# A new order for the first third of a cross-attention and quantized feed-forward kernel

## The chip, the cores and the metric

The kernel runs on one core of one Trainium2 chip. A core has a tensor engine (TensorE, PE in the profile; its weight loads are PEld), a vector engine (VectorE, DVE), a scalar engine (ScalarE, ACT), a general engine (GpSimd, POOL) and a sync engine (SyncE, SP), which here issues all transfers. Each takes its own instructions in order; they wait for one another by semaphores. The metric is the time on the device in microseconds, as the median of several runs.

## The reference, cut to what matters

```python
x = x + xattn(layernorm(x), ctx, Wq, Wkv, Wout, bout)   # x: 4 x 2048 x 512, ctx: 4 x 154 x 512
x = x + ffn(layernorm(x), w1, b1, w2, b2, gamma, beta)  # 512 -> 2048 -> 512

# in xattn: 16 heads of 64; query i sees key j only where  j % 2048 == i
sim  = where(mask, q @ k.T * scale, max_neg); attn = softmax(sim)
out  = (attn @ v) @ Wout + bout
# in ffn: h = layernorm(x) * gamma + beta; then twice, around an exact gelu:
xq, sx = round(x * 127 / max|x|), ...           # by row
wq, sw = clip(round(w / mean|w|), -1, 1), ...   # one scale for a whole weight
y = (xq @ wq.T) / (sx * sw) + b
```

Query i < 154 sees exactly one key, its own, so its attention output is v of that key; a query from 154 on sees none, all its scores are alike, and its output is the mean of all v. The attention thus adds to x, in each batch, 154 different rows and then one row over and over. The weights of the feed-forward part become -1, 0 and 1, and the mean of |w| must be known before any of them can be made.

## The kernel before, in words

x is 64 tiles of 128 rows. They are numbered n in the order in which they are worked: in a batch the tiles 2 to 15 (which only get the mean row) come first, then tile 0 (`front`) and tile 1 (`second`). Everything is written out by hand, instruction by instruction, in three strings of words: BEGINNING (up to tile 23), STEADY (one round for four tiles, eight times) and ENDING (the last eight tiles). No planner runs; each word calls a small function, in the order of the string, and so sets the order on the queue of each engine. A word is letters and numbers; the table `words` near the end maps them. The ones that the text speaks of:

- `lo`, `lv`: load a block of Wout and of Wv (256 KB each, eight each). `w c`: eight instructions on TensorE that add block c of Wv times Wout into four banks; after `w7` the product W is complete, and `cw k` copies a quarter of it to SBUF (last number 1: VectorE, 0: ScalarE).
- `lc`: load the context (1232 KB). `sk k` sums its keys, `sf` spreads the first batch's mean, `mk` writes the means beside the last 26 keys of each batch, `lk` copies those keys.
- `pm`: mean row of batch 0 times W (bank `py_mean`); `Y b`: the first 128 keys of batch b times W (`py`); `pr`: the other keys and the means times W (`py_rest`). Each comes in two halves such as `Y0.0.2` and `Y0.2.4`, of four instructions (two blocks of K in f32). `y b`, `m` and `yr` read these banks on VectorE. The banks come from a pool of two (`ps_o`), which `W`, the second product of the feed-forward part, uses as well.
- `lw i.c`: load block c of w1 (i = 0) or of w2 (i = 1), 512 KB each, eight each. `ms i.c.v` sums its absolute values (v = 1 VectorE, 0 ScalarE), `z i.0` adds the eight sums, `z i.1` spreads the total by a product with ones on TensorE, `z i.2` makes the scale. `q i.c.v` turns a block into whole numbers, `c i.c.v` clips it to -1 to 1 (v = 1 VectorE, 0 GpSimd).
- `L i`: load a pair of x tiles. `lr`, `lb`: rows of bout, gamma, beta, b2 and halves of b1, spread over the partitions.
- For a tile n: `A`/`a` adds the attention's rows to x (VectorE / GpSimd); `S` takes mean and variance; `O`, `o`, `C` or `N` the reciprocal deviation of a group of tiles (`o` and `N` on GpSimd); `P`, `E` (VectorE) or `k`, `e` (GpSimd) or `P`, `g` the normalized rows; `R` their largest value and scale; `V`/`v` scales with w1's (`inv`, the "1 / d" by which b1 is multiplied); `Q` quantizes on ScalarE and `T` turns the tile by a transposing transfer on SP's queue.
- `I n.h.v`: the seed: half h of b1 times `inv` is written into the PSUM half in which the product then accumulates (v = 1 VectorE, 0 ScalarE). `U n`: the first product, 16 instructions of TensorE, 3.45 us. `G`: gelu of a half on ScalarE; `M`: its largest value on VectorE; `H`: quantization on ScalarE; `h`: the turn, on SP's queue; `W n`: the second product, 16 instructions; `D`, `X`/`x`, `F`, `f`: scale, b2, finish and store.

The PSUM halves of `I`, `U` and `G` come from a pool of three (`ps_h`), so a tile's second half is seeded only when a gelu of the tile before has read its own. The x pairs and the loaded blocks of w1 and w2 share a pool of 13 buffers (`ring`). An instruction's place on its queue is fixed; nothing overtakes.

Up to tile 0's product TensorE's order is `w0` to `w7` (with `z0.1` ahead of `w6`), `pm`, `Y0.0.2`, `Y2.0.2`, `Y0.2.4`, `z1.1`, `Y2.2.4`, `Y3.0.2`, `U0`, `Y3.2.4`, `U1`, `Y1` and `pr` by halves in turn, `U2`, `U3`, `W0`, `U4`, `W1`, `U5`, `W2`, `W3`, `U6`, `U7`, `W4`. The pieces that the change touches are these three strings alone; no function changes.

## Time and profile before

| | us |
|---|---|
| median of four runs (lowest, highest) | 513.13 (512.58, 513.32) |
| time of the profiled execution | 513.14 |
| its span | 511.0 |
| TensorE busy | 500.7 |
| VectorE, ScalarE, GpSimd busy | 424.5, 422.9, 390.6 |
| first product of tile 0 starts | 53.31 |
| last product ends, before the last finish and store | 506.99 |

The profile is of one execution. A row of the order of time has the start and the length in us, the engine, the line of the kernel, the operation, what it writes and reads (`out<-in`), the shape, how many instructions are merged in the row, and in brackets how long the engine stood idle before it and what ended that. TensorE's matmuls are pipelined and their ends modelled, so its slow stretches are read from the distances between weight loads and from the granted clock. An f32 product counts as two instructions per block of K. The function that all of TensorE's attention products share is line 470; `U` is line 560, `W` line 638, the seed line 552 (ScalarE) or 550 (VectorE), the whole numbers line 247 or 245, the clip line 250.

### The profile page before, as it was taken

The page shows a single profiled execution, that of the slowest core. Times are in us where ns is not written, and L with a number is a line of the kernel's source. Part 1 is how long each engine was busy: PE and PEld are TensorE (multiplying, and loading weights), DVE is VectorE, ACT ScalarE, POOL GpSimd, SP SyncE. Part 2 cuts the span into 40 slices and gives each one's busy share as a digit, 9 for nine tenths or more (in the row PEclk, how much of TensorE's full clock was granted, in tenths as well). Part 3 has the DMA queues.
Part 4 walks back from the last instruction along what each step waited for, and adds up shares of the span by engine and source line. Part 5 has one row for each costly group of instructions (what it writes and reads, how often), then busy time and mean ns, then how long its engine had stood idle before and what let it go on. Part 6 is the DMA issues. An engine that isn't in the chain of part 4 may idle for free.

```text
span 511.0 us, 6841 instructions
## 1 busy us (share of the span) xinstructions
PE 500.7 (98%) x2168; PEld 224.4 (44%) x2168; DVE 424.5 (83%) x768; ACT 422.9 (83%) x389; POOL 390.6 (76%) x499
## 2 busy tenths in 40 slices
PE   9997999999999999999999999999999999999996
PEld 3443444444444444444444444444444444444442
DVE  1388999898998999889899897989897989796751
ACT  1267999898998999898897997988888889989870
POOL 0049999999999999998998989798989788804020
PEclk9997999999999999999999999999999999999999
DMA  8998698566787976685978776968778694684644
GB/s 294 401 390 313 239 220 135 127 151 153 161 207 168 234 172 139 139 195 137 182 188 174 188 166 158 198 149 183 178 157 212 158 148 126 125 204 100 151 96 144
DMA packets 194111, 93.99 MB, mean 184 GB/s; under 512 B 170268, under 2 KB 170268, under 8 KB 194076
## 3 DMA queue, kind: packets, MB, share of 16 engines
q1 hardware_dynamic: 194076, 93.56, 75.7%
q8 instruction: 17, 0.28, 0.2%
q14 instruction: 18, 0.15, 0.1%
HBM read 34.55 MB, written 17.04 MB: 101 GB/s over the span
## 4 chain that ended last, share of the span: by engine, by line
PE 74%; POOL 13%; DMA 6%; DVE 3%; issue 1%; SPq 1%; ACT 1%; POOLq 0%; ACTq 0%; DVEq 0%
PE po L638 37%; PE ph L560 34%; POOL x L274 3%; DMA wo<-Wout_dram 3%; PE wps L441 2%; DMA x<-x_dram 1%; POOL h L331 1%; POOL h L332 1%; POOL w2q L250 1%; DMA hqT<-hq 1%; POOL r L297 1%; POOL x L354 1%; POOL h L328 1%; DVE m L591 1%; PE py_mean L470 1%
## 5 line engine op out<-in xcount | busy, mean ns | idle before, releaser
L560 PE MATMUL ph<-w1q,xqT 128*128 128x512 f16 x1024 | 230.2, 379 | 1.8 <-DVE ph L550 1.0
L638 PE MATMUL po<-w2q,hqT 128*128 128x512 f16 x1024 | 229.9, 379 | 0.5 <-DVE x L644 0.4
L591 DVE TENSOR_REDUCE m<-hid 128x1 f32<-128x1024 f32 (+1 forms) x130 | 152.7, 1191 | 30.8 <-ACT hid L579 30.6
L579 ACT ACTIVATE hid<-ph,d 128x1024 f32<-128x1024 f32 (+1 forms) x130 | 140.0, 1090 | 32.6 <-PE ph L560 25.1
L560 PEld LDWEIGHTS <-xqT 128*128 128x128 f16 x1024 | 100.1, 98 | 124.2 <-issue 4.3
L638 PEld LDWEIGHTS <-hqT 128*128 128x128 f16 x1024 | 99.9, 98 | 122.2 <-DMA hqT<-hq 1.7
L620 ACT ACTIVATE hq<-hid,i 128x2048 f16<-128x2048 f32 (+1 forms) x65 | 127.5, 1969 | 6.5 <-DVE i L608 1.9
L552 ACT ACTIVATE ph<-b_b,inv 128x1024 f32<-128x1024 f32 x92 | 101.4, 1113 | 2.3 <-POOL inv L374 0.8
L354 POOL TENSOR_TENSOR x<-x,b_b 128x512 f32<-128x512 f32 x58 | 72.8, 1271 | 0.0
L274 POOL TENSOR_TENSOR x<-x,mean 128x512 f32<-128x512 f32 x50 | 63.9, 1281 | 1.0 <-DVE mean L685 1.0
L332 POOL TENSOR_TENSOR h<-h,beta_b 128x512 f32<-128x512 f32 x46 | 58.8, 1279 | 3.6
L644 DVE SCALAR_TENSOR_TENSOR x<-po,d,x 128x512 f32<-128x512 f32 x64 | 47.4, 742 | 13.9 <-PE po L638 12.8
L331 POOL TENSOR_TENSOR h<-h,gamma_b 128x512 f32<-128x512 f32 x46 | 58.4, 1269 | 0.3
L613 POOL TENSOR_TENSOR d<-mh,wm 128x1 f32<-128x1 f32 x64 | 12.1, 192 | 56.7 <-DVE mh L606 52.8
L380 ACT ACTIVATE xqg<-h,s 128x512 f16<-128x512 f32 x64 | 45.3, 711 | 6.4 <-DVE s L368 3.1
L550 DVE TENSOR_SCALAR ph<-b_b,inv 128x1024 f32<-128x1024 f32 x36 | 45.8, 1271 | 0.0
L360 DVE TENSOR_REDUCE m<-h 128x1 f32<-128x512 f32 x64 | 41.6, 671 | 4.1 <-POOL h L332 3.9
L281 DVE BATCH_NORM_STATS2 bn<-x 128x6 f32<-128x512 f32 x64 | 43.4, 677 | 0.4 <-POOL x L274 0.4
L328 POOL TENSOR_SCALAR h<-x,minus,rstd 128x512 f32<-128x512 f32 x46 | 36.7, 801 | 1.1
L441 PE MATMUL wps<-wo,wv 128*128 128x512 f32 x64 | 29.4, 616 | 0.1
L250 POOL TENSOR_SCALAR w1q<-wi 128x1024 f16<-128x1024 int16 x5 | 5.3, 1060 | 29.9 <-ACT wi L247 27.3
L256 DVE TENSOR_REDUCE part<-ws 128x1 f32<-128x1024 f32 x6 | 7.0, 1212 | 18.9 <-DMA ws<-w1T_dram 18.9
(77 smaller groups left out, 289.7 us busy)
## 6 DMA issues: line engine op xcount, KB each, us to landing
x<-x_dram SPq DMA_DIRECT2D x32, 512.0 KB, 4.3
out_dram<-x SPq DMA_DIRECT2D x64, 256.0 KB, 2.4
ws<-w1T_dram SPq DMA_DIRECT2D x8, 512.0 KB, 8.1
ws<-w2T_dram SPq DMA_DIRECT2D x8, 512.0 KB, 10.1
wo<-Wout_dram SPq DMA_DIRECT2D x8, 256.0 KB, 8.1
wv<-WvT_dram SPq DMA_DIRECT2D x8, 256.0 KB, 3.4
ctx_sb<-ctxT_dram SPq DMA_DIRECT2D x1, 1232.0 KB
hqT<-hq SPq DMA_TRANSPOSE x65, 4.5
```

The lines of the kernel that those rows point to most:

```text
L274: e.tensor_tensor(x_of(n), x_of(n), y, ALU.add)
L331: nc.gpsimd.tensor_tensor(normed[n], normed[n], gamma_b, ALU.mult)
L332: nc.gpsimd.tensor_tensor(normed[n], normed[n], beta_b, ALU.add)
L354: e.tensor_tensor(x_of(n), x_of(n), b2_b, ALU.add)
L550: nc.vector.tensor_scalar(ph, row, d, None, ALU.mult)
L552: nc.scalar.activation(ph, row, AF.Identity, bias=0.0, scale=d)
L560: nc.tensor.matmul(bank[i], xqT[n][:, k, :], w1q[:, k, i * 512 : (i + 1) * 512], start=False, stop=(k == KD - 1), skip_group_check=True,)
L579: nc.scalar.activation(hidden[n][:, i * w : (i + 1) * w], up_ps[n][half][:, lo : lo + w], AF.Gelu, bias=0.0, scale=deq1[g][:, j : j + 1],)
L591: nc.vector.tensor_reduce(m2[:, i : i + 1], hidden[n][:, i * w : (i + 1) * w], AX.X, ALU.max, apply_absolute_value=True,)
L620: nc.scalar.activation(hq[n][:, lo : lo + w], hidden[n][:, lo : lo + w], AF.Identity, bias=0.0, scale=inv2[n],)
L638: nc.tensor.matmul(po, hqT[n][:, k, :], w2q[:, k, :], start=(k == 0), stop=(k == KH - 1))
L644: nc.vector.scalar_tensor_tensor(t, down_ps.pop(n), deq2[n], t, ALU.mult, ALU.add)
```

## The change

Only the order is other. In words:

- The w1 blocks come as 7, 3, 2, 0, 6, 4, 1, 5 instead of 5, 2, 6, 1, 3, 7, 4, 0. One block of w2 (5) is loaded ahead of w1's last, the context one block of Wv later, both halves of b1 ahead of tile 0's turn. w1's blocks are measured three on VectorE and five on ScalarE (five and three before).
- Seven of w1's eight clips are on GpSimd (four before) and two of W's quarters are copied by VectorE (none before). `mk` stands behind tile 0's sum `A0` (ahead of the mean `m` before).
- `Y3` is whole ahead of tile 0's product, and so is `pr`; `Y1` lies by halves behind tiles 0 and 1, `Y2` behind tile 2.
- Behind w2's scale, ScalarE makes five blocks of whole numbers (four before) ahead of tile 0's seeds `I0.0.0` and `I0.1.0`, and tile 1's `Q1` comes behind the second seed (between the two before).
- From tile 4 on, `U` and `W` alternate on TensorE (before, `W2 W3 U6 U7` and a few such pairs later). Some tiles change engine: `A18 A28 A29 A30 A34` become `a`, `a24 a31` become `A`, tiles 16, 18, 21 and 26 go by `P`, `g` instead of `k`, `e`, and tile 29 the other way.
- STEADY has its words in another order, with `U` and `W` alternating, and its `P`, `k`, `e` and `g` one tile on; ENDING has `D`, `H` and `X` at other places in the first three tiles.

```diff
     BEGINNING = """
-        lo0 lv0 lo1 lv1 lo2 lw0.5 lw0.2 lv2 lv3 w0 lw0.6 lw0.1 lo3 lv4 lw0.3 w1 ms0.2.1
-        lv5 lo4 ms0.5.1 lw0.7 w2 lw0.4 lw0.0 lo5 lv6 w3 lo6 lr0 lc lv7 w4 ms0.4.1 lo7
-        ms0.1.1 ms0.0.0 L0 lr1 ms0.3.1 ms0.7.0 w5 lw1.0 lw1.6 ms0.6.0 L1 z0.0 z0.1 w6 z0.2
-        q0.5.1 q0.4.0 lw1.2 sk2 lw1.5 q0.6.0 c0.4.0 sk0 lw1.7 sk1 q0.1.0 c0.6.0 w7 q0.3.1
-        lw1.4 xo0 q0.7.0 lw1.3 sk3 sf cw0.0 lw1.1 c0.3.1 cw1.0 c0.1.1 q0.0.1 lr2 pm0.2
-        cw3.0 lk q0.2.1 cw2.0 c0.7.1 ms1.0.0 L2 c0.2.0 pm2.4 ms1.6.1 ms1.2.0 lr3 c0.0.0 mk
-        Y0.0.2 m ms1.5.0 L3 A0 a3 S0 Y2.0.2 ms1.7.0 lb0 O0 P0 o0 ms1.4.0 a2 C0 Y0.2.4 S3
-        ms1.3.0 a1 S2 ms1.1.0 O2 c0.5.0 S1 O1 E0 o1 o2 z1.0 R0 z1.1 a5 Y2.2.4 z1.2 Q0 C1
-        a4 q1.5.0 T0 y0 a6 q1.4.0 O3 lb1 C2 Y3.0.2 q1.0.0 P1 V0 o3 E1 q1.1.0 a7 R1 I0.0.0
-        S4 c1.4.0 Q1 S5 X1 I0.1.0
-        U0 T1 C3 P3 q1.6.0 V1 L4 N4 L5 E3 L6 I1.0.0 L7 P2 Y3.2.4 L8 end G0.0 E2 k4 R2 G0.1
-        e4 M0.0 I1.1.0
-        U1 R3 Q2 G1.0 T2 y2 k5 y3 q1.3.0 Y1.0.2 V2 M0.1 a8 G1.1 L9 L10 pr0.2 V3 I2.0.0 S6
-        e5 R4 Q3 Y1.2.4 M1.0 I2.1.0 T3 a11 S8 H0 pr2.4 R5 c1.1.0 S7 h0
-        U2 I3.0.0 c1.0.0 M1.1 q1.7.0 a10 G2.0 yr c1.3.0 sr q1.2.0 I3.1.1 c1.7.0
-        U3 L11 Q4 c1.2.0 v4 y1 G2.1 T4 D0 N6 c1.5.1 c1.6.1 H1 P6 W0 M2.0 I4.0.0 a9 h1 M2.1
-        G3.0 a12 t1 I4.1.0
-        U4 S9 s0 k7 S10 Q5 N8 x0 H2 T5 P9 E6 W1 G3.1 D2 h2 e7 M3.0 G4.0 M3.1 I5.0.0 D1 g9
...
-        U5 F0 R6 H3 R7 k8 M4.0 V6 Q6 h3 e8 W2 F1 G4.1 S11 I6.0.0 T6 S12 X6 Q7 R8 f0 G5.0
-        T7 R9 X2 W3 M4.1 G5.1 f1 D3 a14 Q8 I6.1.0 M5.0 a17 H4 M5.1
-        U6 X4 N10 I7.0.0 A23 h4 F2 G6.0 x3 T8 H5 I7.1.1
...
+        lo0 lv0 lv1 lo1 lv2 lw0.7 lw0.3 lo2 lo3 w0 lw0.2 lv3 lw0.0 lo4 ms0.7.0 lw0.6 w1
+        ms0.3.1 lv4 lo5 lv5 w2 lw0.4 lv6 ms0.0.1 lw0.1 lw1.5 w3 ms0.6.0 lw0.5 lo6 lv7 lc
+        w4 ms0.4.1 lo7 lr0 ms0.1.0 L0 ms0.2.0 w5 L1 ms0.5.0 lw1.2 lr1 z0.0 lw1.0 z0.1 w6
+        z0.2 q0.7.1 q0.6.0 q0.4.1 q0.1.0 c0.6.0 sk0 lw1.6 lw1.3 sk1 q0.3.0 c0.1.0 lw1.1 w7
+        sk2 c0.7.0 q0.2.0 sk3 lw1.4 sf q0.5.0 c0.2.0 cw0.1 c0.4.0 lk cw1.0 lw1.7 pm0.2
+        cw2.0 xo0 ms1.5.1 q0.0.0 lr2 L2 cw3.1 pm2.4 c0.3.0 ms1.2.0 c0.5.1 c0.0.0 L3
+        ms1.0.0 Y0.0.2 m lb1 ms1.6.0 A0 a3 mk S0 Y0.2.4 L4 ms1.3.0 O0 P0 o0 ms1.1.0 lb0 a2
+        S3 Y3.0.2 C0 ms1.4.0 lr3 a1 S2 ms1.7.0 O2 S1 o2 E0 z1.0 R0 z1.1 a5 O1 Y3.2.4 Q0
+        z1.2 o1 P1 q1.2.0 T0 V0 P2 a7 q1.7.0 O3 y0 q1.0.0 C1 a4 pr0.2 C2 q1.6.0 o3 E1
+        q1.1.0 c1.7.0 R1 pr2.4 I0.0.0 E2 V1 c1.1.0 S4 I0.1.0
+        U0 S5 a6 Q1 R2 q1.5.0 T1 X1 y3 I1.0.0 C3 a8 Y1.0.2 end G0.0 yr N4 P3 I1.1.0 E3
+        U1 Q2 c1.5.1 S6 G0.1 T2 c1.0.0 R3 G1.0 L5 V2 M0.0 L6 k4 Y1.2.4 I2.0.0 e4 M0.1 Q3
+        q1.4.0 T3 M1.0 I2.1.0
+        U2 L7 k5 y1 e5 G1.1 v3 S7 H0 S8 Y2.0.2 N6 R4 I3.0.0 h0 c1.4.1 Y2.2.4 c1.6.1 M1.1
+        G2.0 k7 q1.3.0 c1.2.0 I3.1.1
+        U3 H1 D1 a9 R5 M2.0 c1.3.0 Q4 W0 G2.1 T4 P6 D0 V4 a10 G3.0 S9 sr h1 M2.1 I4.0.0
+        a14 Q5 N8 E6 I4.1.0
+        U4 s0 x0 T5 G3.1 P9 t1 F0 a11 I5.0.0 L8 y2 W1 H2 D2 R6 k8 M3.0 e7 G4.0 S10 h2 S11
...
+        U5 X2 R7 f0 G4.1 L9 M3.1 V6 Q6 e8 I6.0.0 T6 W2 M4.0 H3 F1 a12 M4.1 G5.0 h3 X4
+        I6.1.0
+        U6 F2 g9 Q7 S12 G5.1 T7 M5.0 N10 H4 s1 P10 W3 x3 M5.1 I7.0.0 h4 a13 G6.0 D3 R8 k11
+        f1 H5 I7.1.1
...
     STEADY = """
-        W-3
-        U0 I1.0.1 a12 S11 G0.0 N8 I1.1.0 M0.0
-        U1 Q2 P9 G0.1 T2 k8 G1.0 M0.1 k7 W-2 X3 I2.0.1 I2.1.0 G1.1 e7 F-3 Q3 f-3 H0 T3
...
+        U0 G0.0 W-3 I1.0.1 I1.1.0 G0.1 M0.0 Q2
+        U1 F-3 k7 T2 I2.0.1 X2 L14 G1.0 M0.1 e7 W-2 G1.1 R6 M1.0 I2.1.0 a13 R7 H0 a12 S11
...
     ENDING = """
-        U0 I1.0.1 k7 e7 W-3 G0.0 G0.1 M0.0 D-1 X1 I1.1.0 M0.1
...
+        U0 I1.0.1 G0.0 W-3 k7 G0.1 M0.0 e7 I1.1.0 M0.1 Q2
...
```

## The prediction

> **What bounds the kernel now.** I read the page's busy shares first, then the waits and the order of time of TensorE, then the stretches where it stands still.
>
> ```profile
> PE 500.7 (98%) x2168; PEld 224.4 (44%) x2168; DVE 424.5 (83%) x768; ACT 422.9 (83%) x389; POOL 390.6 (76%) x499
> ```
>
> TensorE is the bound: 98% busy, and the change adds and removes no product. Only time in which TensorE waits or runs slowly can be won or lost. TensorE in order of time, its bracketed idle times:
>
> ```profile
> 45.45 2.05 PE L230 MATMUL pt<-tot,ones 128*128 128x512 f32 x2 [2.87 <-DVE tot L224]
> ...
> 53.31 3.61 PE L560 MATMUL ph<-w1q,xqT 128*128 128x512 f16 x16 [0.35 <-ACT ph L552]
> ...
> 100.54 1.89 PE L560 MATMUL ph<-w1q,xqT 128*128 128x512 f16 x8 [0.44 <-ACT ph L552]
> 103.47 1.89 PE L560 MATMUL ph<-w1q,xqT 128*128 128x512 f16 x8 [1.05 <-DVE ph L550]
> ...
> 119.57 3.61 PE L638 MATMUL po<-w2q,hqT 128*128 128x512 f16 x16 [0.40 <-DVE x L644]
> ```
>
> The busy time by stretches (columns: stretch, length, PE, PEld, DVE, ACT, POOL, granted clock, DMA share, GB/s):
>
> ```profile
> 42.60:45.40 2.80, 0.00 (x0) 0.00 (x0) 2.66 (x9) 2.23 (x4) 2.59 (x3) 0.86 1.05 402
> 45.40:51.50 6.10, 6.05 (x7) 2.53 (x8) 4.59 (x16) 4.23 (x5) 6.10 (x8) 0.50 0.64 216
> ```
>
> The wait of 2.87 us for w2's total (z1.1) costs twice: behind it the clock is 0.50 for 6.1 us, which loses another 3.05. With 0.66 at 23.2 (weight loads 1.09 apart where 0.43 is usual, ending on a landing of Wout), 0.35 ahead of tile 0, 1.49 at tile 7 and 0.40 at 119.6, 8.8 us can be won at most. From 120 on TensorE has no gap. What it waits for in the front stands here (VectorE, ScalarE, GpSimd in order of time):
>
> ```profile
> 36.39 0.89 DVE L460 TENSOR_SCALAR ctx_rest<-sums 128x16 f32<-128x16 f32 x1
> 45.16 0.15 DVE L224 TENSOR_REDUCE tot<-part 128x1 f32<-128x8 f32 x1
> ```
> ```profile
> 43.85 1.06 ACT L262 ACTIVATE w2q<-ws 128x1024 f16<-128x1024 f32 x1 [0.17 <-DMA ws<-w2T_dram]
> ...
> 47.99 4.27 ACT L247 ACTIVATE wi<-ws,sw 128x1024 int16<-128x1024 f32 x4 [0.89 <-DVE sw L238]
> 52.16 1.10 ACT L552 ACTIVATE ph<-b_b,inv 128x1024 f32<-128x1024 f32 x1
> ```
> ```profile
> 35.09 2.15 POOL L250 TENSOR_SCALAR w1q<-wi 128x1024 f16<-128x1024 int16 x2 [2.65 <-DVE wi L245]
> 38.25 1.28 POOL L274 TENSOR_TENSOR x<-x,mean 128x512 f32<-128x512 f32 x1 [1.01 <-DVE mean L685]
> ```
>
> The last measured block of w2 lands at 43.85; the total follows at 45.16, behind an unbroken row of VectorE work.
>
> **The change part by part.**
>
> *Loads on SP's queue.* Waits show w1's last block landed at 22.50, Wout's sixth at 23.21, the context at 28.39: 0.65 us per 256 KB. The new order has w5's pair six such units earlier, so the 0.66 goes. But a block of w2 and the fifth w1 block now end w1's set four units later: 22.5 + 2.6 = 25.1, then 1.25 to measure (1.06 and the 0.19 read) and 0.16 for the total: 26.6. Before, that total ended at 25.92, with TensorE there at 26.75. The product z0.1 stays at about 26.75: nothing gained, and 0.2 lost at worst. The context lands 1.3 later (29.6); its four sums (0.74 each) and the spread (0.6) end at 33.2, then VectorE copies W's first quarter (cw0.1; the copies on ScalarE take 0.53, I take 0.6): 33.8, where TensorE is ready at 33.84. +0.06. Ahead of w2's last block stand 15,056 KB in both orders, so it lands at 43.85 again. Behind that block tile 0's turn (T0) had 8 units ahead of it on SP's queue (beta, b2, two x pairs, one half of b1); now it has 12 (both halves and a third pair): 43.85 + 12 x 0.67 = 51.9, and 2.4 to 2.7 us of its own, 54.6 at the latest. The seed below comes later, so it is hidden; without that cover it would cost 1.3 against 53.3. SP stands at T0 until 47.9, and behind it lie only T1 and later x pairs.
>
> *w1's clips.* GpSimd gets seven of eight instead of four (1.04 each), done at about 37.3: covered, since tile 3's sum (a3) waits for the mean until 38.3 anyway. Without that cover, 1 us of GpSimd.
>
> *mk, the mean of the keys.* It moves behind tile 0's sum, next to a3. Its row has 0.89 us for 16 elements and ends with the clip of GpSimd's row above (37.24). I read it as held by GpSimd: here until a3's end at 39.6, so tile 0's statistics start 0.9 later (39.7). Bounds: 0.15 (the small rows) to 1.3 (a whole a3). I take 0.9, from where a3 stands in the row. The Trainium skill, SBUF — State Buffer, section "SBUF: two separate sides", says VectorE's two-port operations and GpSimd lock one port pair for a whole instruction; by that rule lk and the clip c0.5.1, now beside GpSimd's clips, would wait up to 1.04 each too: all of it ahead of the mean at 37.5, so the sum stays.
>
> *The chain to z1.0.* Behind it o0 ends at 41.9, a2 and a1 (1.24 each) at 44.4, tile 1's statistics (0.82) and tile 0's affine (0.67) at 45.94. w2's total is then at 45.94 instead of 45.16, TensorE's z1.1 at 46.2 instead of 45.45. The products ahead of it are as many as before, so the wait grows to some 3.6. The clock came back at 51.5 before; if at the same moment, 0.4 of its loss returns. The Trainium skill, TensorE: Matmul & The Clock Gate, Part 1, halves the clock after an idle window of about 3.4 us; here 2.8 sufficed. By the rule alone only the longer wait would surely halve it, which adds nothing to a clock already halved.
>
> *Five blocks ahead of b1 / d.* w2's scale follows z1.1 by 2.5 us: 48.7. ScalarE then makes five blocks instead of four (1.04 each) and tile 0's first seed (1.04): 55.0 instead of 53.2. Tile 0's product starts at 55.1 instead of 53.31: +1.8.
>
> *The products of the rest.* Behind z1.1 and ahead of tile 0 stood two half products (Y2.2.4, Y3.0.2: four instructions each); now three (Y3.2.4, pr0.2, pr2.4). The third is 4 x 0.43 = 1.72 us of work that is no longer owed later (two of Y2 move behind tile 2 for it and for Y1's). pr0.2 needs the bank that y0 frees at about 50.9 and would be next at 50.7: 0.2, hidden too, since TensorE is done at 54.9 and the seed comes at 55.0. Net at tile 0: 1.8 - 1.72 = +0.1. If mk is not held, ScalarE is 0.8 earlier and TensorE itself the limit at 54.4: -0.6.
>
> *Up to tile 7.* Y1 and Y2 lie behind tiles 0, 1 and 2, so tile 2 comes 3.4 us earlier against its own inputs; its second seed ends at 67.4, needed at 67.2: +0.3. From 48.7 ScalarE has 8 blocks (1.04), 11 seeds (1.04), 10 gelus (1.0), 5 x (0.62) and 3 h (1.89): 38.7, to 87.7. GpSimd, from a3 at 38.3: 12 sums (1.24), 4 powers (3.5), 5 clips (1.02), scales 2.3, b2 1.24, 3 norms (3.0), 3 k/e (3.4) and a k, 0.5: 47.5, and 2.35 idle: tile 7's normal rows at 88.2, before 87.18:
>
> ```profile
> 85.94 1.27 POOL L332 TENSOR_TENSOR h<-h,beta_b 128x512 f32<-128x512 f32 x1
> ```
>
> TensorE now alternates W and U: W2, U6, W3, U7 where it had W2, W3, U6, U7. U6 is due at 93.4, three earlier, and its scales come at 89.3 to 90.4, its turn at about 93.5. ScalarE waits some 2 us at Q6 for them, and behind it on that queue stand both seeds of tile 6, h of tile 3 and a gelu: it seeds the second half by 95.7 (wait 0.5); h of tile 3 at 93.6 and 4.5 us (the row below, turns from issue to landing) give W3 at 98.1 (wait 0.6). In return tile 7 finds both seeds, its 1.49 is gone, and it ends at about 105.1 where it ended at 105.2. The later 0.40 hangs on a finish behind a held GpSimd; it may stay.
>
> ```profile
> DMA to landing us min/median/max: 4.2/4.5/5.7
> ```
>
> *The rest.* From tile 8 on three more tiles go by VectorE and GpSimd together (P, g), three sums cross back, the steady rows shift a P, k, e and g by one tile and the ending's two dequants wait for their words. TensorE's order at the end is the same, so the last 4.0 us are. I cost all this at nothing: other engines are 87 to 91% busy in that stretch, TensorE 100%. If that cover fails, one late seed (1.1) in each of eight steady rounds would be 9; nothing points there.
>
> **Sum.** Profiled 513.14 (span 511.0 and 2.1 around), 0.01 off the median. +0.1 at tile 0, +0.3 at tile 2, +0.4 -0.9 at tiles 6 and 7 (to -0.1 at 105), and half of the 0.40, -0.2: -0.3 at the lowest and +0.1 with the h of W3 at the longest landing of the row (5.7). I forecast 513.0, no change. 0.2% (1.03 us) is about what a measurement tells.
>
> **The rivals.**
>
> *Slower: tiles 6 and 7 find ScalarE and the turns late.* Place: U6 and W3, from 93 to 102. For it: ScalarE starts w2's blocks 0.8 later and GpSimd ends tile 7's rows 1.0 later, while U6 is due 3.1 earlier. Against: seeds and h by the list are only 0.5 late. It decides once U6's turn lands later than about 95. With scales at 90.4 and the longest landing of an x turn (5.5), U6 starts at 96.5, 3.1 late; tile 7 ends at 107 with W3 hidden: +1.8, so 514.9. If such a stand halves the clock again, as 2.87 did, 3 more: 517.9.
>
> *Faster: alternation wins.* mk is not held (-0.7 at tile 0), tile 2's seed is in time, U6 and W3 start as due (92.4 and on): tile 7 ends at 102.7, -2.5, and 0.4 at 119.6: 510.2. For it: 1.49 of the gaps arise in two products back to back with three halves of PSUM. Against: GpSimd's and ScalarE's sums above.
>
> *The change does not do what it says:* pr was hidden ahead of U2 anyway, so its move would only shift when TensorE waits; that is inside the likeliest case.
>
> **How the numbers follow.** No change beyond 0.2%: 0.40 (512.1 to 514.1). Slower by tile 6 or by a longer front: 0.34. Faster: 0.26. The range leaves out a tenth at each end: from 511.0, most of the way to the faster rival, to 516.4, half way between the two prices of the slower one.
>
> **What would show it.** mk at about 0.8 beside a3; w2's total near 45.9 and z1.1's wait near 3.6; clock 0.50 behind it; tile 0's product at 55.1 with little idle; no pair of U products; waits of about half a microsecond at U6 and W3 in place of 1.49 at tile 7. Wrong if w2's total is early enough to keep the clock (-6), or if TensorE stands more than 2 us anywhere behind tile 0.

## The result, and the profile after

The changed kernel takes 514.07 us in the median of 42 runs (511.75 to 516.41), the kernel before 512.98 beside it (60 runs, 512.12 to 513.75): a ratio of 1.0022, 95% interval 1.0015 to 1.0030. That is 0.8 to 1.5 us slower, where no change was forecast. What is new is the spread: 4.7 us, where the kernel before has 1.6. The profiled execution took 511.85, almost the shortest of all, so its page alone shows a gain; the loss has to be read from other executions (below).

The busy share, then TensorE in order of time (start, length, line, operation, idle time before it and what ended that):

```profile
PE 498.4 (98%) x2168; PEld 223.8 (44%) x2168; DVE 421.3 (83%) x761; ACT 426.5 (84%) x392; POOL 391.8 (77%) x505
```
```profile
45.53 1.22 PE L233 MATMUL pt<-tot,ones 128*128 128x512 f32 x2 [3.32 <-DVE tot L227]
46.54 3.50 PE L473 MATMUL py<-w_sb,ctx_sb 128*128 128x512 f32 x4
49.88 3.60 PE L473 MATMUL py_rest<-w_sb,ctx_rest 128*128 128x512 f32 x8
53.61 3.61 PE L563 MATMUL ph<-w1q,xqT 128*128 128x512 f16 x16
...
66.58 1.89 PE L563 MATMUL ph<-w1q,xqT 128*128 128x512 f16 x8 [0.74 <-ACT ph L555]
...
91.35 3.63 PE L641 MATMUL po<-w2q,hqT 128*128 128x512 f16 x16 [1.95 <-DMA hqT<-hq]
...
105.17 1.03 PE L641 MATMUL po<-w2q,hqT 128*128 128x512 f16 x4
```

Tile 7's wait of 1.49 and the 0.40 at 119.6 are gone; in their place stand 0.74 at tile 2's second half and 1.95 at W2, the second product of tile 2. The row at 105.17 is W4, behind tile 7's first product; before it started at 105.20. The stretches (columns as in the forecast: PE, PEld, DVE, ACT, POOL, granted clock, DMA share, GB/s):

```profile
42.20:45.50 3.30, 0.01 (x1) 0.00 (x1) 2.79 (x9) 2.12 (x4) 2.12 (x4) 1.00 1.05 396
45.50:49.70 4.20, 4.17 (x6) 1.78 (x7) 3.71 (x14) 3.18 (x4) 4.20 (x6) 0.60 1.04 405
```

The wait for w2's total grew by 0.45, yet the clock behind it was low for a shorter time than before: 0.60 over 4.2 us, so at half for 3.4 of them, where the kernel before had at least the 6.1 of its row. What TensorE waits for (VectorE, ScalarE, GpSimd, and SP's queue, whose rows give the time of issuing):

```profile
38.30 0.89 DVE L463 TENSOR_SCALAR ctx_rest<-sums 128x16 f32<-128x16 f32 x1
...
45.23 0.15 DVE L227 TENSOR_REDUCE tot<-part 128x1 f32<-128x8 f32 x1
...
47.06 1.40 DVE L349 SCALAR_TENSOR_TENSOR h<-x,mv,gamma_b 128x512 f32<-128x512 f32 x2
...
48.44 0.68 DVE L518 TENSOR_TENSOR front<-py,bout_b 128x512 f32<-128x512 f32 x1
```
```profile
47.24 5.31 ACT L250 ACTIVATE wi<-ws,sw 128x1024 int16<-128x1024 f32 x5
52.46 2.13 ACT L555 ACTIVATE ph<-b_b,inv 128x1024 f32<-128x1024 f32 x2
```
```profile
37.87 1.27 POOL L277 TENSOR_TENSOR x<-x,mean 128x512 f32<-128x512 f32 x1 [0.84 <-DVE mean L688]
...
87.46 1.27 POOL L357 TENSOR_TENSOR x<-x,b_b 128x512 f32<-128x512 f32 x1
```
```profile
82.83 0.55 SPq L528 DMA_DIRECT2D mean<-rest_dram  x1
83.44 0.42 SPq L200 DMA_DIRECT2D x<-x_dram  x1
84.14 5.14 SPq L634 DMA_TRANSPOSE hqT<-hq  x1
```
```profile
DMA to landing us min/median/max: 7.2/7.2/7.2
```

`mk` (38.30) is held until `a3` (37.87 to 39.14) ends, as forecast. Five blocks and two seeds follow w2's scale. Tile 7's normal rows end on GpSimd by 87.5, where the row shown follows them, not at 88.2. The last row is the turn of the hidden rows in the stretch from 75 to 95; in the same stretch of the kernel before it is 4.4. The turn at 84.14 is tile 2's, behind the spread of a mean row (`t1`) and an x pair (`L8`); its issue alone took 5.14.

**Behind tile 7.** The same product is reached at 115.56 before and 115.53 after, at 119.57 and 118.99, and the last merged row of products starts at 493.01 and 491.95. So 0.58 comes from the wait at 119.6. The other 0.48 are small pauses in the repeated rounds, which in the trace of before are rows of two products that last 7.36, 7.15 and 7.18 (at 271.52, 299.43, 410.02) where others last 7.07. They do not belong to the order: the profiled execution of e3 below has the rounds of the kernel before, no such rows, and takes 372.96 us from the product at 119.93 to the last merged row at 492.89, as long as the changed kernel (118.99 to 491.95). The time from W4 to the end of the execution is 407.9 before, 407.5 in e3 and 406.7 after; in the profiled executions of the changed kernel's other orders it is 406.6 to 406.8, however late they reach W4, but 407.1 in e7 and 407.4 in e13. The median loss of 1.1 is therefore a loss of some 2 us ahead of W4, in a typical execution, less 0.6 to 1.1.

**Executions differ by where the clock falls.** Sorted by their mean granted clock (54 executions of the changed kernel, with those of the next section; 126 of the kernel before beside four of the five sets of experiments):

| mean clock | changed: number, median (range) | before: number, median (range) |
|---|---|---|
| under 0.9945 | 18, 514.98 (513.94 to 516.41) | 24, 513.01 (512.39 to 514.83) |
| 0.9945 to 0.9975 | 31, 513.71 (511.85 to 515.45) | 73, 513.13 (511.94 to 514.81) |
| over 0.9975 | 5, 512.39 (511.75 to 512.81) | 29, 513.01 (512.41 to 513.92) |

The kernel before shows no loss where the mean clock is lower; the changed one is 2.6 us slower in the first row than in the last. Within the middle row it still spreads over 3.6 us, so the length of the half clock alone does not sort its executions. 25 of its 54 executions took over 514.2, and 5 of 126 before. The task of the experiments is to find what the kernel before had to hide it, and where the changed one shows it.

### The profile page after: what moved, and what is told of

Read it like the earlier page. It is cut to its first block, busy times and chain, and to the rows that moved or that the text cites. A ratio compares the mean times of both kernels' runs of the same rounds, so it can differ in the third digit from the quotient of the medians.

```text
span 509.9 us, 6878 instructions
## 1 busy us (share of the span) xinstructions
PE 498.4 (98%) x2168; PEld 223.8 (44%) x2168; DVE 421.3 (83%) x761; ACT 426.5 (84%) x392; POOL 391.8 (77%) x505
## 4 chain that ended last, share of the span: by engine, by line
PE 81%; DMA 1%; DVE 0%; issue 0%; DVEq 0%
PE po L641 42%; PE ph L563 39%; DMA hqT<-hq 1%; DVE x L647 0%; DVEq L647 0%
## 5 line engine op out<-in xcount | busy, mean ns | idle before, releaser
L582 ACT ACTIVATE hid<-ph,d 128x1024 f32<-128x1024 f32 (+1 forms) x130 | 141.7, 1095 | 34.7 <-PE ph L563 33.4
L555 ACT ACTIVATE ph<-b_b,inv 128x1024 f32<-128x1024 f32 x91 | 100.0, 1110 | 1.4 <-POOL inv L377 0.6
L357 POOL TENSOR_TENSOR x<-x,b_b 128x512 f32<-128x512 f32 x59 | 74.8, 1271 | 0.0
L277 POOL TENSOR_TENSOR x<-x,mean 128x512 f32<-128x512 f32 x53 | 67.0, 1272 | 2.0 <-DMA x<-x_dram 1.2
L335 POOL TENSOR_TENSOR h<-h,beta_b 128x512 f32<-128x512 f32 x43 | 54.5, 1268 | 3.4
L553 DVE TENSOR_SCALAR ph<-b_b,inv 128x1024 f32<-128x1024 f32 x37 | 47.1, 1273 | 0.2 <-ACT hid L582 0.2
L331 POOL TENSOR_SCALAR h<-x,minus,rstd 128x512 f32<-128x512 f32 x43 | 33.1, 770 | 0.3
L253 POOL TENSOR_SCALAR w1q<-wi 128x1024 f16<-128x1024 int16 x7 | 7.5, 1095 | 26.8 <-ACT wi L250 26.7
L299 POOL TENSOR_SCALAR a<-mv 128x4 f32<-128x4 f32 (+2 forms) x17 | 4.8, 282 | 20.6 <-DVE mv L285 20.0
```

What stands on the lines that cost most here:

```text
L277: e.tensor_tensor(x_of(n), x_of(n), y, ALU.add)
L335: nc.gpsimd.tensor_tensor(normed[n], normed[n], beta_b, ALU.add)
L357: e.tensor_tensor(x_of(n), x_of(n), b2_b, ALU.add)
L553: nc.vector.tensor_scalar(ph, row, d, None, ALU.mult)
L555: nc.scalar.activation(ph, row, AF.Identity, bias=0.0, scale=d)
L582: nc.scalar.activation(hidden[n][:, i * w : (i + 1) * w], up_ps[n][half][:, lo : lo + w], AF.Gelu, bias=0.0, scale=deq1[g][:, j : j + 1],)
```

## The experiments

All but two are the changed kernel with one or more steps moved or added. Results, each against the kernel before on the same chip (the ratio is of the mean times). e1 to e4, e5 to e8, e9 to e12, e13 to e16, and e17 with e18 ran on five chips, and the unaltered changed kernel was run beside the first set alone, so medians of different sets are compared across chips:

| run | edit | median (range), us | ratio (95%) |
|---|---|---|---|
| e1 | none | 513.98 (511.76 to 515.04) | 1.0009 (0.9996, 1.0023) |
| e2 | z1.1's wait filled | 512.78 (511.92 to 513.17) | 0.9987 (0.9978, 0.9996) |
| e3 | the kernel before, wait filled | 513.02 (512.66 to 514.52) | 0.9998 (0.9988, 1.0009) |
| e4 | four blocks ahead of the seed | 515.05 (513.16 to 515.70) | 1.0026 (1.0014, 1.0039) |
| e5 | W2's wait filled | 514.04 (511.94 to 515.25) | 1.0015 (1.0003, 1.0027) |
| e6 | `t1` behind the turn | 512.69 (511.78 to 515.66) | 1.0001 (0.9987, 1.0015) |
| e7 | `L8` behind the turn | 513.61 (511.61 to 514.46) | 1.0001 (0.9988, 1.0014) |
| e8 | both | 514.76 (513.35 to 515.95) | 1.0031 (1.0018, 1.0045) |
| e9 | `y0` early | 513.31 (512.30 to 515.02) | 1.0011 (0.9998, 1.0024) |
| e10 | `pr` back behind tile 1 | 516.87 (515.56 to 517.43) | 1.0069 (1.0054, 1.0083) |
| e11 | the kernel before, new STEADY and ENDING | 512.64 (512.28 to 513.87) | 0.9994 (0.9983, 1.0004) |
| e12 | e9 and z1.1's wait filled | 512.92 (512.25 to 515.94) | 1.0001 (0.9988, 1.0013) |
| e13 | e9 and e7 | 512.59 (511.29 to 513.51) | 0.9993 (0.9982, 1.0003) |
| e14 | e9 and e5 | 512.97 (511.98 to 514.17) | 1.0000 (0.9989, 1.0011) |
| e15 | e2 and e7 | 512.13 (511.27 to 515.16) | 0.9988 (0.9974, 1.0002) |
| e16 | e13 and `mk` early | 512.00 (510.67 to 513.38) | 0.9985 (0.9972, 0.9998) |
| e17 | e16 and z1.1's wait filled | 512.84 (511.34 to 514.43) | 0.9998 (0.9988, 1.0008) |
| e18 | `mk` early | 512.87 (512.01 to 514.19) | 1.0002 (0.9993, 1.0012) |

### Is it the clock? (e1 to e4)

e1 is the changed kernel once more; e2 and e3 add three products of ones by ones, whose result is overwritten, to TensorE ahead of z1.1's product; e4 takes the fifth block behind the seeds.

```diff
             if i:
                 pt = ps_h.tile([P, 1024], F32, tag="ph", name=f"pt_{i}")[:, :512]
+                for _ in range(3):
+                    nc.tensor.matmul(
+                        pt, ones, ones.unsqueeze(1).to_broadcast([P, 4, P]), start=True, stop=True
+                    )
```
```diff
-        q1.1.0 c1.7.0 R1 pr2.4 I0.0.0 E2 V1 c1.1.0 S4 I0.1.0
-        U0 S5 a6 Q1 R2 q1.5.0 T1
+        c1.7.0 R1 pr2.4 I0.0.0 E2 V1 S4 I0.1.0
+        U0 S5 a6 Q1 q1.1.0 c1.1.0 R2 q1.5.0 T1
```

> The changed kernel once more, unaltered. Two theories. CLOCK: the executions of the changed kernel lie between 511.75 and 516.41 because the half clock behind z1.1's wait lasts about 3.4 us in some (mean granted clock 0.997) and 7 us in others (0.993), and the delay is handed on to w2's scale and tile 0's seeds. Then the times sort by clock: 0.993 at about 515.2, 0.997 at about 513, and the kernel before has 0.993 in nearly all executions, within 513.8. TURNS: the spread comes from late turns of h between 85 and 100 us (W2 waited 1.95 us in the profile), whatever the clock; then both clocks show the same spread, and the wait at W2 or W3 differs by 2 us or more from that of the first profile.

> Three products of ones with ones (six f32 instructions, 2.6 us at full clock) in the changed kernel ahead of the spread of w2's total, so that TensorE stands idle some 0.7 us there in place of 3.3. CLOCK: the clock stays 1.00 behind it in every execution, the mean clock is 0.999 or more, the spread shrinks below 1.5 us and the median falls by 2 us or more, to 510.5 to 512. TURNS: the clock is kept, but the median falls by less than 1.5 us and the spread stays near 4 us, since W2 still waits.

> The same three products in the kernel before, where the wait was 2.87 us. CLOCK: the half clock of 6.1 us goes (3.05 us lost) and w2's scale comes 1 us earlier (its product took 2.05 us at half clock, 1.0 at full), so the median falls by 1 to 3 us, to 510 to 512, and is then close to that of the filled changed kernel or below it. TURNS: no change beyond 0.5 us, since tile 0's first seed and later the engines other than TensorE set the time in both.

> The changed kernel with four whole-number blocks ahead of tile 0's seeds, as before the change; the fifth and its clip follow Q1. By my step the first seed ends 1.04 us earlier and TensorE, not the seed, is the limit at tile 0; what tile 0 gains (0.7 or less) ScalarE owes again by tile 2, whose second seed is where it was. CLOCK: median within 0.7 us of the changed kernel's and the same spread. If the fifth block is what made the change slower: 1 us or more faster than the changed kernel, 513 or below.

Filling keeps every execution of e2 at a clock of 0.998 or more and takes the spread from 3.3 to 1.25 us and the median below the kernel before; the median fell by 1.2 us, within TURNS's 1.5 and short of the 2 or more that CLOCK expected. Filling changes more than the front, though: in e2 W1 waits 1.28 us for its turn, and W2 for none, and so it is in all filled orders of the changed kernel (1.77, 1.81 and 1.75 in e12, e15 and e17), while W1 has no such wait in the others. Why is open. In the kernel before, filling (e3) gains nothing, against CLOCK's 1 to 3 us: its tile 0 waits 2.18 us for ScalarE's seed instead, and then runs at half clock itself:

```profile
52.76 5.30 PE L564 MATMUL ph<-w1q,xqT 128*128 128x512 f16 x16 [2.18 <-ACT ph L556]
```

So in the three profiled executions of the kernel before's front, tile 0 starts when its seed is there, whether a half clock lies ahead of it (0.35 us of waiting, 0.68 in e11) or not (2.18). The instruction that frees the bank for `Y3.0.2` stands ahead of the affines there:

```profile
48.42 0.68 DVE L515 TENSOR_TENSOR front<-py,bout_b 128x512 f32<-128x512 f32 x1
...
49.70 0.74 DVE L346 SCALAR_TENSOR_TENSOR h<-x,mv,gamma_b 128x512 f32<-128x512 f32 x1
```

Not so in the changed kernel. In e4's profiled execution (515.12), where the fifth block is out of the way, TensorE in order of time, and VectorE:

```profile
46.55 2.05 PE L233 MATMUL pt<-tot,ones 128*128 128x512 f32 x2 [3.32 <-DVE tot L227]
48.39 2.40 PE L473 MATMUL py<-w_sb,ctx_sb 128*128 128x512 f32 x4
52.79 5.37 PE L473 MATMUL py_rest<-w_sb,ctx_rest 128*128 128x512 f32 x8 [1.99 <-POOL r L317]
57.99 3.62 PE L563 MATMUL ph<-w1q,xqT 128*128 128x512 f16 x16
```
```profile
48.91 3.07 DVE L349 SCALAR_TENSOR_TENSOR h<-x,mv,gamma_b 128x512 f32<-128x512 f32 x2
...
51.97 0.67 DVE L518 TENSOR_TENSOR front<-py,bout_b 128x512 f32<-128x512 f32 x1
```

Tile 0 starts at 57.99 and waits for no seed. The way there: z1.1's product takes 2.05 instead of 1.22; `z1.2` on VectorE comes later, and so do `P1` and `P2` behind it; these now start after GpSimd's two sums have begun, beside which they last 3.07 instead of 1.40; `y0` stands behind them and frees its bank 6.1 us after z1.1's product began (52.64 - 46.55) instead of 3.6 (49.12 - 45.53); the half product of the rest has waited 1.99 us for that bank, long enough to have the clock halved again (5.37 where 3.60 is usual). (The row names GpSimd's `r` as what ended the wait; that ends at 52.67, but no product reads it; `y0`, which ends at 52.64, is what reads the bank.) e5 and e6 show the same row of events in their profiled executions: a product of 1.94 and 2.05, a pair of 3.20 and 3.08, a wait of 1.75 and 1.89. From z1.1's product to tile 0's it is 8.1 us in the profile above, 9.8 in e5 and 11.4 in e4 and e6. Where the clock stays up (e2, e7, e8, e18) TensorE waits for the bank too, 0.80 to 0.99 us, but then another 0.48 to 0.68 for the seed, so the bank costs nothing there. e4, e5 and e6 also began z1.1's product 0.5 to 1.0 us later than the profile above, as the first product `Y0` did (37.44 to 37.92 for 36.90); so late is `Y0` in e8 and e13 too, and no run here explains it. The fifth block is not the cause: e4 is as slow as any, 1.1 us over e1 where at most 0.7 was expected.

### The second place: W2 (e5 to e8)

e1's profiled execution (515.04) has tile 0 near its time at 53.83, but this at W2:

```profile
92.84 5.31 PE L641 MATMUL po<-w2q,hqT 128*128 128x512 f16 x16 [2.12 <-DMA hqT<-hq]
```
```profile
92.80:97.90 5.10, 5.06 (x16) 2.02 (x17) 2.46 (x6) 5.04 (x6) 4.68 (x5) 0.67 0.98 232
```

The wait is hardly longer than in the profile above (1.95), but here the clock is halved behind it and W2 takes 5.1 instead of 3.45 us. That is 1.7 of the 3.2 us by which e1 reaches W4 later; 1.3 were lost by tile 5's product (87.11 for 85.78), in short waits for banks and for a clipped block. e5 fills this wait with two products of ones, e6 to e8 take `t1`, `L8` or both behind the turn on SP's queue:

```diff
         po = down_ps[n] = ps_o.tile([P, D], F32, tag="po", name=f"po_{n}")
+        for _ in range(2 if n == 2 else 0):
+            nc.tensor.matmul(
+                po, ones, ones.unsqueeze(1).to_broadcast([P, 4, P]), start=True, stop=True
+            )
```
```diff
-        U4 s0 x0 T5 G3.1 P9 t1 F0 a11 I5.0.0 L8 y2 W1 H2 D2 R6 k8 M3.0 e7 G4.0 S10 h2 S11
+        U4 s0 x0 T5 G3.1 P9 F0 a11 I5.0.0 y2 W1 H2 D2 R6 k8 M3.0 e7 G4.0 S10 h2 t1 L8 S11
```

> Two f32 products of ones with ones (1.7 us) ahead of W2 alone, in the wait of about 2 us that W2 has for its turned h. Theory SECOND GATE: in the slower executions of the changed kernel that wait halves the clock once more, and W2 then takes 5.2 us instead of 3.5; nothing behind it can give that back. Then the executions with clock 0.993 at 514 and more thin out, the mean clock is 0.997 or more, the spread falls below 2 us and the median falls by 1 to 1.7 us, to 512.3 to 513. Rival FRONT: the slow executions come from the wait at z1.1 and its half clock; then the median and the spread stay (513.9 to 514.2, over 3 us).

> The changed kernel with t1 (the second batch's mean row, read 128 times from one row of the device's memory) behind h2 instead of ahead of it on SP's queue. Theory QUEUE: h2 takes 7.2 us from its quantization to the product because it stands behind t1 (7.3 us from issue to landing in the kernel before); with t1 behind it the wait at W2 falls from 2 us to below 0.5, and the median falls by 1.5 us or more, to 512.5 or below, with clocks of 0.997 and more. Rival LATE H: the quantization of tile 2's h itself ends too late (84.1, the product due at 89.4); then the wait stays above 1.5 us and the time as it is.

> The changed kernel with L8 (a pair of x tiles, 512 KB) behind h2 instead of ahead of it, t1 as it was. QUEUE, if the bytes count and not t1's single row: the wait at W2 falls by about 1.3 us (512 KB at 390 GB/s) and the median by 0.7 to 2 us. If t1 is what counts: no change, within 0.5 us.

> t1 and L8 both behind h2. QUEUE: no wait at W2 (below 0.3 us), median 511.5 to 512.5, spread below 2 us: faster than both kernels. LATE H: no change.

e5 alone does nothing for the median, as FRONT expected: six of its twelve executions took over 514.2, and the profiled one of these lost most of its time in the front (tile 0 at 55.84). e6 cuts the wait at W2 to 0.22, as QUEUE expected, and its median fell by 1.3 us, but three executions stayed over 514.2. e7 shortens the turn's issue from 5.14 to 2.89, and W2 no longer waits, but tile 6's product then waits 0.69 for its turned rows, and the median fell by less than the 0.7 expected. With both moved (e8) that wait is 2.83, and 2.17 in e6: what is put behind the turn pushes the next one back. e8 missed both expectations, with 514.76.

```profile
84.09 2.89 SPq L634 DMA_TRANSPOSE hqT<-hq  x1
87.02 0.58 SPq L200 DMA_DIRECT2D x<-x_dram  x1
```

In the kernel before `t1` and `L8` are issued a round and four rounds earlier, a turn in this stretch lands in 4.4 us and W2 has no wait. Either place alone explains only part of the long executions, so the question became whether both together explain all of them.

### The bank and the place of the rest's products (e9, e10, e12)

e9 takes `y0` to where VectorE waits for z1.1's product anyway; e12 adds the three products of ones to it; e10 undoes the move of `pr`.

```diff
-        S3 Y3.0.2 C0 ms1.4.0 lr3 a1 S2 ms1.7.0 O2 S1 o2 E0 z1.0 R0 z1.1 a5 O1 Y3.2.4 Q0
-        z1.2 o1 P1 q1.2.0 T0 V0 P2 a7 q1.7.0 O3 y0 q1.0.0 C1 a4 pr0.2 C2 q1.6.0 o3 E1
+        S3 Y3.0.2 C0 ms1.4.0 lr3 a1 S2 ms1.7.0 O2 S1 o2 E0 z1.0 R0 z1.1 a5 y0 O1 Y3.2.4 Q0
+        z1.2 o1 P1 q1.2.0 T0 V0 P2 a7 q1.7.0 O3 q1.0.0 C1 a4 pr0.2 C2 q1.6.0 o3 E1
```
```diff
-... C1 a4 pr0.2 C2 ... R1 pr2.4 I0.0.0 ... G0.0 yr N4 ... L5 V2 M0.0 ... M1.0 I2.1.0 U2 L7 k5 y1
+... C1 a4 C2 ... R1 I0.0.0 ... G0.0 N4 ... L5 pr0.2 V2 M0.0 ... M1.0 pr2.4 I2.1.0 U2 L7 k5 yr y1
```

> After, with tile 0's front rows (y0) taken on VectorE ahead of the first opening of the norm, so straight behind z1.1's statistics, where VectorE waits for z1.1's product anyway; nothing else moves. The theory that y0's place is what hurts (BANK): the half product of the rest no longer waits for its bank (0.56 to 1.99 us before), TensorE is idle for 0.6 to 2 us less ahead of tile 0, which starts at 53.4 to 54.5 in every execution instead of 53.4 to 58.0; median about 512.9 (0.9 to 1.2 under the changed kernel's 514.0), slowest below 514.8. Rival (CLOCK): the half clock behind the long wait for w2's total does the harm by itself; without the wait for the bank the products of the rest start earlier, still at half clock, and tile 0 waits for its seeds; median within 0.4 of 514.0, and executions of 515 remain.

> After, with the products of the rest of the rows taken back behind tile 1's product, by halves as they were (and their sum with b_out behind the second half). BANK: tile 0 no longer depends on y0 or on the clock at which the products of the rest run; it starts at its seeds, 53.3 to 54.5, but the wait ahead of it is long (near 4 us) and it runs at half clock for some time, as the kernel before does when z1.1's wait is filled (5.30 us for 3.4); the 3.4 us of products then stand in the way of tile 2: median 513.2 to 513.6, with executions closer together than the changed kernel's 4.7 us. Rival (the move is harmless, the second gate at tile 2's down-projection and the order behind make the loss): median 514 or more, same spread.

> After, with y0 early as in the first run of this call, and three products of ones by ones (each about 1.1 us, nothing is read from them) ahead of z1.1's product, which keep TensorE's clock up through the wait for w2's total. BANK and CLOCK together: wait for w2's total under 0.6 us, no wait for the bank, tile 0 waits 1 to 2 us for its seeds (53.6 to 54.5); median 512.3 to 512.6, 0.2 to 0.5 under the run with the filling alone (512.78), and under the kernel before by 0.6 to 0.9. Rival: with both gone the idle time gathers ahead of tile 0 in one piece of over 2 us and halves the clock there, as it did in the kernel before with filling; then 513 or more.

e9's profiled execution (514.93) had the slowest sort of front, a product of 2.04 and half clock up to 51.8, and still its TensorE did not wait for the bank and began tile 0 9.05 us after z1.1's product, where e4, e5 and e6 took 9.8 to 11.4. Against the profile above it lies 1.2 us back at tile 5's product, and W2's half clock adds 1.7:

```profile
45.83 2.04 PE L233 MATMUL pt<-tot,ones 128*128 128x512 f32 x2 [3.31 <-DVE tot L227]
...
51.08 3.96 PE L473 MATMUL py_rest<-w_sb,ctx_rest 128*128 128x512 f32 x8
54.88 3.62 PE L563 MATMUL ph<-w1q,xqT 128*128 128x512 f16 x16
...
92.74 5.31 PE L641 MATMUL po<-w2q,hqT 128*128 128x512 f16 x16 [2.17 <-DVE m L594]
```

Five of twelve executions remained at 514.9 to 515.0; between them and 513.5 there is nothing. So the bank theory held for the front's wait, and missed the median (513.31 for 512.9); in the one of these five that was profiled the second place remained.

e10 missed both expectations: 516.87. Without the products of the rest, TensorE waits 3.44 us for tile 0's seed, and tile 0 runs at half clock (5.30) from 55.08. Against e9, whose front has a like clock, tile 5's product starts 4.3 us later (91.24 for 86.95), of which e9 gives 2.3 back at its W2. In the median undoing the move costs 2.9 us against e1. So in this order the move of `pr` was no harm: it is work where TensorE would stand, and the place of `y0` spoiled it. e12 shows the same from the other side: with `y0` early and the wait filled, the idle time gathers ahead of tile 0 (2.08 us), and nothing is won over e2. It missed its 512.3 to 512.6, and the clock was not halved behind that wait, as the rival had it.

### What lies behind tile 7 (e11)

> The kernel before with the changed kernel's orders of the repeated groups of four tiles and of the last eight (from tile 24 on), its own front. If what lies behind tile 7 is worth what the profiles show (406.7 against 407.9 us from tile 7's product to the end): 1.0 to 1.2 us faster, 511.9 to 512.2. If that difference belongs to tiles 8 to 23, which are written out with the front, or is the state that the front leaves: within 0.4 of 513.1.

e11 has BEGINNING of the kernel before and STEADY and ENDING of the changed one. Its mean is 0.3 us lower (interval -0.9 to +0.2), no difference that can be told from none, and less than the 1.0 to 1.2. The 0.58 at 119.6 belongs to BEGINNING (its wait stands here at 119.01, 0.39 long), at the seam of the two orders a product waits 0.51 at 221.55, and by e3 the rounds had nothing to win.

### Both places at once (e13 to e16)

```diff
-        ms1.0.0 Y0.0.2 m lb1 ms1.6.0 A0 a3 mk S0
+        ms1.0.0 mk Y0.0.2 m lb1 ms1.6.0 A0 a3 S0
```

e13 is e9 with e7's edit, e14 is e9 with e5's, e15 is e2 with e7's, e16 is e13 with the edit shown.

> After with y0 early, and the load of the ninth pair of x's tiles (L8) behind the turn of tile 2's hidden rows instead of ahead of it on SP's queue, so that the turn's issue takes some 2.9 us instead of 5.1. If the slow group is made at tile 2's down-projection (W2): W2 waits under 1 us, no half clock there, the group near 515 is gone; median 512.5 to 513.0, slowest under 514. If it is made in the front: four or five in twelve remain at 514.5 to 515, median as with y0 early alone (513.3).

> After with y0 early, and two products of ones by ones (about 1.7 us, overwritten) ahead of W2. W2 theory: the turn still lands as late, W2 starts at the same time but at full clock, 3.45 instead of 5.1 us; the group near 515 is gone, median 512.8 to 513.2. Front: unchanged, 513.3 and a group near 515.

> After with three products of ones by ones ahead of z1.1's product, and L8 behind the turn of tile 2's hidden rows. Both cures together: no half clock in the front and no wait at W2; median 512.2 to 512.5, 0.3 to 0.5 under the filling alone, and 0.6 to 0.9 under the kernel before. If W2's wait only moves on (to tile 6's product, which then waits for its turned rows, as when both queue steps were moved): 512.8, as with the filling alone.

> As e13, with the mean's columns of the rest's key matrix (mk, held 0.89 us by GpSimd's add beside it) written ahead of tile 0's sums, where VectorE waits 0.96 us for them anyway. If the statistics behind mk set w2's total, as the prediction's step says: total at 44.4 to 44.8 instead of 45.2 to 45.5, TensorE's wait 2.4 to 2.8 instead of 3.3, tile 0 0.4 to 0.9 earlier; median 0.3 to 0.8 under e13, so 511.9 to 512.6. If the statistics wait for GpSimd's adds instead: the same as e13.

Executions over 514.2 us, by what was mended:

| | W2 as it is | W2 filled | turn earlier (`L8`) |
|---|---|---|---|
| front as it is | 25 of 54 | 6 of 12 | 1 of 12 |
| `y0` early | 5 of 12 | 0 of 12 | 0 of 12 |
| front filled | 0 of 11 | | 1 of 12 |

With `y0` early and W2 mended the long executions are gone, in both ways of mending the second; `y0` alone or the filling of W2 alone leaves as large a share as there was. That fits two places, and the rows above show both, but the counts do not prove that these are all: e2, e12 (1 of 11) and e15 have few or none with the wait moved to W1, and e18 below has none over 514.2, though two at 514.18 and 514.19, with neither place mended. The medians of e13, e14 and e16 came out within what was expected, e15's a little under it; yet its profiled execution waits 1.81 us at W1. e14's profiled execution still has the half clock in front (2.05 for z1.1's product, tile 0 at 55.07) and a late turn, and took 513.08. `L8` alone left one long execution of twelve, fewer than the front's half clock would let one expect; twelve are too few to say why.

e16 is the best order found: 512.00, by its interval 0.1 to 1.4 us under the kernel before, with no work added. It was the best of many, so its interval flatters it.

```profile
45.74 1.59 PE L233 MATMUL pt<-tot,ones 128*128 128x512 f32 x2 [2.77 <-DVE tot L227]
...
94.70 3.63 PE L563 MATMUL ph<-w1q,xqT 128*128 128x512 f16 x16 [1.25 <-DMA xqT<-xqg]
```

### mk alone, and the filled best (e18, e17)

> After with mk alone written ahead of tile 0's sums. If the 0.9 us that mk is held beside GpSimd's add passes through the statistics to w2's total: wait for the total 2.8 instead of 3.3, median 0.4 to 0.8 under the changed kernel (513.98 and 514.07), so 513.2 to 513.7, and a slow group at 514 to 515 stays, because y0's place and W2's wait are as they were. If mk's place only counts where the other two are mended: 513.8 to 514.3.

> The run with y0 early, L8 behind the turn and mk ahead, with two products of ones by ones (about 2.2 us, nothing is read from them) ahead of z1.1's product. If the clock in the front still costs: no half clock there, executions closer together, median 511.4 to 511.9. If the seeds' cover already hides it: 512.0 as without filling, or up to 0.6 more if the idle time gathers ahead of tile 0 to over 2 us and halves the clock there.

With `mk` alone ahead of tile 0's sum, w2's total comes 7.57 us after the start of the mean row `m` (37.30 to 44.87), and 8.13 in the changed kernel (37.10 to 45.23): 0.56 earlier, as the wait shows (2.76 for 3.32). The median is 512.87, more than the 0.4 to 0.8 expected, no execution is over 514.2, and its profiled one still has W2 at half clock:

```profile
45.17 1.10 PE L233 MATMUL pt<-tot,ones 128*128 128x512 f32 x2 [2.76 <-DVE tot L227]
...
91.69 5.31 PE L641 MATMUL po<-w2q,hqT 128*128 128x512 f16 x16 [2.09 <-DMA hqT<-hq]
```

Tile 0 started at 53.12 there, with full clock all through the front, and the execution with the half clock at W2 then ends at 513.88 instead of 515. Filling on top of e16 (e17) did not help: 512.84, on another chip, against both expectations. Two products do not hold the clock: in the profiled execution it is 0.50 from 47 to 50 us behind a wait of 1.89. There w2's total was late (46.02) because VectorE waited 0.93 us for the row of beta to land, and W1 waited 1.75 for a turn. That this is what the filling costs isn't shown.

## Why the prediction was wrong

- **"pr0.2 needs the bank that y0 frees ... hidden too ... net at tile 0 +0.1".** This step failed. Its cover was the seed at 55.0. In fact w2's scale was ready at 47.1 rather than 48.7, since z1.1's product came 0.7 earlier and took 1.22, and the seed was there at 53.6. And `y0`'s time was taken from one execution: it hangs, through `z1.2` and the pair `P1`, `P2`, on the clock of z1.1's product. At full clock the wait for the bank is hidden by the seed, as forecast. Where the clock is halved, `y0` comes up to 2.5 us later, the wait of 0.6 to 2.0 us shows, and tile 0 starts up to 3.4 us later than in the profile above, both counted from z1.1's product. In the kernel before, the chain is shorter: there `y0` stood ahead of the affines, and 1.72 us less work stood ahead of tile 0, so that even at half clock TensorE was done by the time of the seed.
- **"h of tile 3 at 93.6 and 4.5 us"**, and W2 without a wait. This step failed. The price of a turn was a median of the whole kernel, and W2 had no term. The turn that W2 needs lands 7.2 to 7.5 us after its issue starts, behind `t1` and `L8` (6.8 and 7.0 in e2 and e12); W2 waits 1.88 to 2.17 in e1, e4, e9, e18 and the profile above, and in e1, e9 and e18 runs at half clock for another 1.7. This was the slower rival's mechanism (a late turn, then the clock) at another place, W2 instead of U6, at 1.9 to 3.9 us instead of 1.8 to 4.8. The forecast waits at U6 and W3 didn't appear in the changed kernel.
- **"8.8 us can be won at most"**, with 3.05 of it from the half clock. Too high for the front: filling that wait in the kernel before (e3) won nothing, since the seed was not there before 52.76, and the idle time and the half clock moved to tile 0. A slow TensorE costs nothing where another engine ends last.
- **"mk ... 0.9 later".** The hold is right (0.89 us, to `a3`'s end), its price on w2's total was 0.56 (e18). The clip `c0.5.1` on VectorE took 0.77 beside GpSimd's, where such a clip took 0.41 in the kernel before; it lay ahead of the mean, as forecast. The total stood at 45.23 instead of 45.94, the wait at 3.32 instead of 3.6. Another part is the loads, forecast to win nothing: w1's z0.1 came at 26.11, not 26.75, and the mean row `m` at 37.10.
- **Five blocks, +1.8 at tile 0.** The count is right (5.22 us to the seed), the starting point was late: +0.3 in the profiled execution. e4 shows that the fifth block isn't what costs.
- **The products of the rest as 1.72 of work done ahead.** Right in sign; undoing it costs 2.9 in the median. So the rival that the move does nothing is excluded, in this order.
- **"The rest ... at nothing", and half of the 0.40.** It won 0.58 at 119.6. Between the two profiles it is 1.06, but the 0.48 in the rounds, where TensorE was taken to be without a gap, are missing in e3 with the same rounds.
- **Tile 2's seed, +0.3:** 0.74. **Tile 7's row, 105.1:** 105.17 in the profiled execution, but near 108.3 in the long ones (108.35 in e1). The first agreement is luck: tile 0 was 1.5 us earlier than forecast, and the wait at W2 that had no term took 1.95.
- **The clock.** The forecast let it come back at the same moment as before. By the granted clock in stretches of 1 us, the half clock lasts 6.8 us in some profiled executions (the kernel before, from 44.6 to 51.4; e9, e14) and 3.4 in others (after, e1, e3), and behind the same wait of 3.32 it began at 46.4 (after), at 45.8 (e1) or not at all (e7). The Trainium skill, TensorE: Matmul & The Clock Gate, Part 1, speaks of a free-running window of about 3.4 us; these lengths agree, one or two of it. So the phase differs from one execution to the next, and the cost of a wait is a spread and not a number. That reading was open to the forecast and wasn't drawn.
- **Sums.** ScalarE's list adds up to 38.5 and ends at 87.2, not 38.7 and 87.7, and GpSimd's to 46.7, not 47.5, which puts tile 7's rows at 87.4, near the 87.5 measured. GpSimd had five of w1's clips before, not four, one of them behind the mean. No other reading above rests on these.

The range (511.0 to 516.4) held the result; its likeliest case was the wrong one, and its upper end came from a late turn at U6 that did not occur.

## What to carry to other kernels

A chain that is hidden in the one profiled execution isn't hidden if its cover or its start hangs on the granted clock: follow each wait of TensorE with its products at half clock too, and put the instruction that frees a bank ahead of work that doesn't need it. A wait of 2 us on TensorE should be priced with and without a halved clock behind it, and filled with real work where there is some, as the products of the rest do here. The price of a transfer is to be taken from its own place on its queue, behind what is issued just ahead of it, and not from a median of the kernel.

## What the runs showed of the hardware that was not expected

- The length of a wait doesn't tell whether the clock is halved behind it. Waits of 2.09, 2.12, 2.17 and 2.18 us were followed by half clock (e18, e1, e9, e3), others of 2.08 (e12), 2.17 (e6), 2.83 (e8) and 3.32 (e7) by none; e7's 3.32 is followed by a clock of 1.00 over the next 8 us. The page of the Trainium skill named above states an idle window of about 3.4 us as the condition; in these runs about 2 was enough in some executions, which that does not allow, and 3.3 too little in others.
- Two affines of 128x512 on VectorE took 1.40 us where they ended about when GpSimd's two sums began, 2.41 and 2.42 where they began 0.1 us ahead of them (e1, e9; the sums took 3.43 and 3.48), and 3.07 to 3.20 where the sums began first (e4 to e6; 2.94 and 2.95, where they take 2.49 behind the affines).
- A turn of 128x2048 f16 took 1.2 to 3.6 us to issue in the kernel before, and landed 4.2 to 5.7 us from the start of its issue where a wait shows it. Behind a spread row and an x pair it took 4.8 to 5.4 to issue and landed after 6.8 to 7.5; behind the x pair alone it took 3.84 (e6), behind the spread row alone 2.75 to 2.98 (e7, e13, e15 to e17).
